# A graph network on one core: the last hidden state summed with its residual on TensorE, and a new order of all engines

## The chip, the core and the metric

The kernel runs on one core of a Trainium2 chip. A core has four compute engines with a queue each: TensorE (PE, matrix products, with weight loads listed apart as PEld), VectorE (DVE), ScalarE (ACT) and GpSimd (POOL). SyncE (SP) issues the DMA transfers. Each engine works its instructions strictly in the order in which the program lists them and waits on semaphores for the others. Products land in PSUM, eight banks of 128 x 512 fp32 numbers; everything else lives in SBUF. The metric is the device time of one execution in microseconds (us), the median of several runs.

## What is computed

The reference, cut to what matters; `x` is 32 x 512 x 128, `adj` 512 x 512, all fp32:

```python
def _chebyshev(adj, x, order):                 # order 3
    def step(carry, _):
        nxt = jnp.einsum('ij,bjc->bic', adj, carry)
        return (nxt, nxt)
    ...
def _L0_gnn_ref(x_1, adj0, adj1, weight_1):
    parts = [x_1[..., None], _chebyshev(adj0, x_1, 3), _chebyshev(adj1, x_1, 3)]
    x_all = jnp.concatenate(parts, axis=3)
    return jnp.einsum('bnik,iok->bno', x_all, weight_1)

def step(h, _):                                # layer 1, five times
    m_in = jnp.einsum('nm,bmd->bnd', in_matrix, h)
    m_out = jnp.einsum('nm,bmd->bnd', out_matrix, h)
    av = jnp.concatenate([m_in, m_out], axis=-1)
    u3 = h @ u3_w.T + u3_b
    z = jax.nn.sigmoid(av @ w3_w.T + w3_b + u3)
    r = jax.nn.sigmoid(av @ w4_w.T + w4_b + u3)
    hv = jnp.tanh(av @ w5_w.T + w5_b + (r * h @ u5_w.T + u5_b))
    h = (1.0 - z) * h + z * hv
    return (h, None)

x = _layernorm(x + _L0_gnn_ref(x, adj, adj, weight_1), axis=-1)
x = _layernorm(x + _L1_gnn_ref(x, adj, adj, ...), axis=-1)
```

Layer 0 adds a graph convolution to `x` and normalises over the 128 channels; its result is called h0. Layer 1 starts from h0, makes five gated steps, adds the last hidden state h to h0 and normalises again. Both adjacency matrices are the same one, so the two halves of each gate's weight are added beforehand.

## The kernel before

The 32 batches go through in 16 pairs q = 0 to 15, two batches b each; pairs are independent. `pair(q, key0)` builds all the work of a pair: `layer0`, five steps s, then the sum with h0, the second normalisation and the store.

A batch's hidden state exists in two layouts. `hT` has the channels on the 128 partitions and the 512 nodes along the free axis: the gates use it. `X` has the nodes on the partitions: it is the stationary operand of the adjacency product, and the layout of h0 and of the output. After each step h is turned from `hT` to `X`. `turn` does it by a 32 x 32 block transpose on DVE (into a `v` tile), eight small DMAs on SP's queue to DRAM (`d`) and one back. Where `by_dma` is false, four transposes of 128 x 128 on PE (`transposes`, into a PSUM bank `bt`) do it. By `ON_PE = {14: 1, 15: 3}` that is the last step of pair 14 and the last three steps of pair 15.

`pair_product` makes the adjacency product of both batches with seven products instead of eight, out of sums that POOL and ACT prepare in an `S` tile; `seven` lists the products and their evictions. `gates` does one step for one batch: r from w4, z from w3, the candidate from w5 and u5. For r and z, DVE adds bias and u3 in PSUM (L705, L712) and ACT applies the sigmoid (L707, L714); DVE forms r*h (L708), ACT applies the tanh (L721). Then h + z*(hv - h) is formed in three steps: DVE subtracts (L724), DVE multiplies (L726), and POOL adds into `hT` (L729). With `quick` true, which is all steps of the last `QUICK = 2` pairs, DVE does that add.

After the last step of a pair that is turned by DMA, POOL adds `X` to h0 (L792). Where PE turned it, DVE adds the PSUM bank to h0 (L797) and the bank is free. `norm` then takes four groups of 128 channels a batch: DVE makes moments (L283, L284), POOL the power -0.5 and the shift in four small instructions (L287 to L290), ACT scales in place (L293); SP stores (L804).

The order of every engine's instructions comes from a list scheduler, `Plan`. Each piece of work names its engine, a booked duration, what it comes after, which buffers it takes and gives back, and a key. Whenever an engine is free in the plan's clock, it takes the ready piece with the lowest key whose buffers are free. Keys are a pair's start `KEYS[q]`, plus 20 for each step, plus small offsets within a step (product 0, u3 5, gates 10, turn 15, final norm 17). `OVERLAP` shortens the booked occupation of DVE, ACT and POOL and lengthens the lateness of the result by as much, so that a result's time stays while the engine is free sooner. `slots` holds the number of buffers of each kind; `inside` bounds the pairs that have been entered.

The booked time of four PE transposes is 0.44 us, and of a product of two 128-column matmuls in layer 0 (L565) also 0.44.

Of the kernel before, what the change touches and what calls it, by code (L numbers as in the profile page):

```python
# [10 lines left out]
AF = mybir.ActivationFunctionType  # L11
# [3 lines left out]
P = 128  # L15
NK = 4
# [7 lines left out]
QUICK = 2  # L24
KEYS = [20.0, 58.0, 80.0, 112.0, 148.0, 180.0, 208.0, 240.0, 272.0, 304.0, 334.0, 366.0, 396.0, 426.0, 464.0, 478.0]
# [18 lines left out]
class Plan:  # L44
# [6 lines left out]
    OVERLAP = {"DVE": 0.08, "ACT": 0.1, "POOL": 0.04}  # L51
# [6 lines left out]
    def __call__(self, engine, us, emit, after=(), take=(), give=(), key=0.0, late=None):  # L58
        late = self.LATE[engine] if late is None else late
        overlap = min(self.OVERLAP.get(engine, 0.0), us / 2)  # L60
        us, late = us - overlap, late + overlap
        op = Op(engine, us, emit, [a for a in after if a is not None], take, give, key, late)
        self.ops.append(op)
        return op
# [62 lines left out]
def gnn_resnorm_kernel(  # L127
# [26 lines left out]
    def tiles(tag, n, shape=(P, N), pool=work):  # L154
# [7 lines left out]
        tT=tiles("tT", 5),  # L162
        U=tiles("U", 2, (P, NK, 2, P)),
        Y=tiles("Y", 4, (P, 2, NK, P)),
        h0=tiles("h0", 4, (P, 2, NK, P)),
        hT=tiles("hT", 8),
        X=tiles("X", 4),
        uT=tiles("uT", 6),
        rh=tiles("rh", 3),
        z=tiles("z", 4),  # L170
        m=tiles("m", 5),
        S=tiles("S", 2, (P, 7, H, P)),
        v=tiles("v", 7),
        two=[None] * 3,
        inside=[None] * 7,
# [98 lines left out]
    def norm(n, name, src_of, dst_of, after, give, key):  # L274

        mv = small.tile([P, n, 2], F32, tag="mv", name=f"mv_{name}")
        rstd = small.tile([P, n], F32, tag="rstd", name=f"rstd_{name}")
        shift = small.tile([P, n], F32, tag="shift", name=f"shift_{name}")
        got = []

        def moments(i):
            st = small.tile([P, 6], F32, tag="st", name=f"st_{name}_{i}")
            nc.vector.bn_stats(st, src_of(i))  # L283
            nc.vector.bn_aggr(mv[:, i, :], st)  # L284

        def power():
            nc.gpsimd.tensor_scalar(rstd, mv[:, :, 1], EPS, None, ALU.add)  # L287
            nc.gpsimd.tensor_scalar(shift, mv[:, :, 0], -1.0, None, ALU.mult)
            nc.gpsimd.tensor_tensor(rstd, rstd, mhalf[:, :n], ALU.pow)
            nc.gpsimd.tensor_tensor(shift, shift, rstd, ALU.mult)  # L290

        def apply(i):
            nc.scalar.activation(  # L293
                dst_of(i), src_of(i), AF.Identity, bias=shift[:, i : i + 1], scale=rstd[:, i : i + 1]
            )

        for i in range(n):
            got.append(plan("DVE", 0.48, lambda i=i: moments(i), after=after, key=key))
        p = plan("POOL", 1.75, power, after=got, key=key)
        over = []  # L300
        for i in range(n):
            last = i == n - 1
            over.append(
                plan("ACT", 0.5, lambda i=i: apply(i), after=[p] + over, give=give if last else [], key=key)
            )
        return over
# [163 lines left out]
    def fit(t, turned):  # L470
        return t.rearrange("p k (s d) -> p k s d", d=R) if turned else t
# [222 lines left out]
    def gates(name, m, h, after, u_done, quick, key):  # L694

        uT = f"uT{name}"
# [16 lines left out]
        t = plan("DVE", 0.75, emit, after=[p2, u_done], give=[("uT", uT)], key=key + 0.5)  # L713
        emit = lambda: nc.scalar.activation(plan[z], plan[pz], AF.Sigmoid)  # L714
        zs = plan("ACT", 0.59, emit, after=[t], give=[("bank", pz)], key=key + 0.5)
# [6 lines left out]
        t = plan("ACT", 0.66, emit, after=[p4], key=key + 0.8)  # L722

# [4 lines left out]
        engine, us = (nc.vector, 0.69) if quick else (nc.gpsimd, 1.27)  # L728
        emit = lambda: engine.tensor_tensor(plan[h], plan[z], plan[h], ALU.add)  # L729
        return plan("DVE" if quick else "POOL", us, emit, after=[t], give=[("z", z)], key=key + 0.8)  # L730

    def pair(q, key0):
# [6 lines left out]
        for s in range(STEPS):  # L739
# [29 lines left out]
            for b in range(2):  # L769
                nm = f"{name}_{b}"  # L770
                Xb = f"X{nm}"
                d = gates(nm, f"m{nm}", h[b], got[b], u_done[b], q >= NP - QUICK, key + 10)
# [5 lines left out]
                else:  # L778
                    bn = f"bt{nm}"
                    emit = lambda bn=bn, hb=h[b]: transposes(plan[bn], lambda k: plan[hb][:, chunk(k)])  # L780
                    take = [("bank", bn)] + ([] if last else [("X", Xb)])
                    t = plan("PE", 0.44, emit, after=[d] + read[b], take=take, give=give, key=key + 15)
                    if not last:
                        emit = lambda bn=bn, Xb=Xb: nc.scalar.copy(plan[Xb], plan[bn])
                        t = plan("ACT", 0.59, emit, after=[t], give=[("bank", bn)], key=key + 15)
# [5 lines left out]
                if by_dma:  # L791
                    emit = lambda b=b, X_new=X_new, y=y: nc.gpsimd.tensor_tensor(  # L792
                        fit(y(), True), X_new(b), fit(y(), True), ALU.add
                    )
                    t = plan("POOL", 1.27, emit, after=[t], give=[("X", Xb)], key=key + 17)
                else:
                    emit = lambda y=y, bn=bn: nc.vector.tensor_tensor(  # L797
                        y(), plan[bn].rearrange("p (k c) -> p k c", k=NK), y(), ALU.add
                    )
                    t = plan("DVE", 0.69, emit, after=[t], give=[("bank", bn)], key=key + 17)  # L800
# [68 lines left out]
```

## Time and profile before

| | |
|---|---|
| median of 3 runs | 1525.26 us (1524.48 to 1526.72) |
| the profiled execution's own time | 1526.63 us |
| span, first to last instruction | 1524.5 us |
| PE matmul / weight loads, busy | 1498.4 / 1034.4 us |
| DVE / ACT / POOL busy | 975.6 / 753.5 / 750.6 us |
| mean granted PE clock | 0.995 |
| chain that ended last, share by engine | PE 90%, DVE 4%, DMA 2% |
| DMA, mean | 85 GB/s, 31.3% of 16 engines |

The profile is of one execution. Its span leaves out some 2 us around the first and last instruction, so that its own time, not the median, belongs to it. L numbers are lines of the kernel. A row of the timeline gives the start from the beginning of the span, the duration, engine, line, operation, output and inputs, the number of instructions merged, and in brackets the engine's idle time before with what ended it. Matmuls are pipelined: a single one's duration is longer than the distance from its start to the next, and the latter is what it costs a busy PE. In a waits row stand the waiting engine and line, what it waited for, total us, times, and the longest.

### The profile page before, as it was taken

Reading aid. Unit: us, or ns where it says so; the run is one execution under the profiler, and the core shown is the slowest. Engines: PE = TensorE matmul, PEld = TensorE weight load, DVE = VectorE, ACT = ScalarE, POOL = GpSimd, SP = SyncE. Lnnn points to the kernel's source line nnn. Section 1 sums busy time; section 2 is a strip of 40 time slices with the busy share of each in tenths; the row PEclk is TensorE's granted clock in tenths of the full one; section 3 lists DMA queues with packets and bytes.
Section 4 is the critical chain, followed back from the end, with each engine's and each line's share of the span. In section 5 each row is a group of like instructions: output and inputs, shape, how many; then the busy total and the mean of one; then the engine's idle time right before and its main releaser. Section 6 shows DMA issues by size and latency. Waiting matters only on the chain.

```text
span 1524.5 us, 20210 instructions
## 1 busy us (share of the span) xinstructions
PE 1498.4 (98%) x6216; PEld 1034.4 (68%) x6216; DVE 975.6 (64%) x2068; ACT 753.5 (49%) x1610; POOL 750.6 (49%) x1068
## 2 busy tenths in 40 slices
PE   8999999999999999999999999999999999999995
PEld 7876676666766766666676766676675776665563
DVE  5457566766666766566666566666676456766766
ACT  3454545454454455455545454555445435554554
POOL 4654354655564554464645464564553464543222
PEclk9999999999999999999999999999999999999998
DMA  3221333243333324243333433224233033233310
GB/s 116 62 71 48 85 90 98 81 108 101 82 99 97 90 79 109 69 105 83 88 92 98 105 103 77 77 82 132 83 84 99 26 83 84 57 102 90 84 42 28
DMA packets 162140, 129.23 MB, mean 85 GB/s; under 512 B 18544, under 2 KB 127088, under 8 KB 162032
## 3 DMA queue, kind: packets, MB, share of 16 engines
q1 hardware_dynamic: 162032, 127.93, 31.3%
q8 instruction: 50, 0.82, 0.2%
q14 instruction: 58, 0.48, 0.1%
HBM read 64.95 MB, written 62.91 MB: 84 GB/s over the span
## 4 chain that ended last, share of the span: by engine, by line
PE 90%; DVE 4%; DMA 2%; SPq 2%; ACT 1%; POOL 1%; issue 1%; ACTq 0%; POOLq 0%; DVEq 0%
PE bank L487 35%; PE bank L700 32%; PE bank L746 8%; PE bank L624 6%; PE bank L565 6%; DMA X<-d 1%; SPq L315 1%; PE bank L423 1%; PE bank L272 1%; DVE bank L724 1%; DVE st L283 0%; DVE z L726 0%; POOL h L792 0%; DVE mv L284 0%; ACT h L293 0%
## 5 line engine op out<-in xcount | busy, mean ns | idle before, releaser
L487 PE MATMUL bank<-T,S 128*128 128x256 f32 x1400 | 345.4, 380 | 0.3 <-ACT m L348 0.2
L487 PEld LDWEIGHTS bank<-T,S 128*128 128x128 f32 x1400 | 264.3, 190 | 99.2 <-ACT m L348 48.7
L729 POOL TENSOR_TENSOR hT<-z,hT 128x512 f32<-128x512 f32 x140 | 177.4, 1270 | 279.0 <-DVE z L726 274.8
L487 PE MATMUL bank<-at,S 128*128 128x256 f32 x880 | 226.8, 381 | 3.8 <-ACT S L467 1.4
L348 ACT COPY m<-bank 128x256 f32<-128x256 f32 x320 | 118.4, 370 | 216.4 <-PE bank L487 215.3
L487 PEld LDWEIGHTS bank<-at,S 128*128 128x128 f32 x880 | 165.3, 190 | 76.6 <-issue 39.7
L352 DVE TENSOR_TENSOR m<-bank,m 128x256 f32<-128x256 f32 x240 | 100.0, 417 | 171.8 <-PE bank L487 106.5
L724 DVE TENSOR_TENSOR bank<-bank,hT 128x512 f32<-128x512 f32 x160 | 110.0, 692 | 117.7 <-ACT bank L721 116.7
L746 PE MATMUL bank<-hT,u3s 128*128 128x512 f32 x320 | 159.8, 593 | 0.0
L700 PE MATMUL bank<-m,w3s 128*128 128x512 f32 x320 | 158.4, 593 | 0.0
L700 PE MATMUL bank<-m,w4s 128*128 128x512 f32 x320 | 158.4, 593 | 0.0
L700 PE MATMUL bank<-m,w5s 128*128 128x512 f32 x320 | 157.9, 593 | 0.0
L700 PE MATMUL bank<-rh,u5s 128*128 128x512 f32 x320 | 157.1, 594 | 0.7 <-DVE rh L708 0.7
L751 ACT ACTIVATE uT<-bank,ub3s 128x512 f32<-128x512 f32 x160 | 109.6, 686 | 81.4 <-PE bank L746 81.1
L705 DVE SCALAR_TENSOR_TENSOR bank<-bank,b4s,uT 128x512 f32<-128x512 f32 x160 | 119.8, 752 | 46.2 <-PE bank L700 42.4
L721 ACT ACTIVATE bank<-bank,hv_b 128x512 f32<-128x512 f32 x160 | 105.4, 660 | 86.6 <-PE bank L700 85.8
L707 ACT ACTIVATE bank<-bank 128x512 f32<-128x512 f32 x160 | 92.9, 582 | 109.2 <-DVE bank L705 108.6
L712 DVE SCALAR_TENSOR_TENSOR bank<-bank,b3s,uT 128x512 f32<-128x512 f32 x160 | 118.8, 751 | 15.5 <-PE bank L700 14.1
L714 ACT ACTIVATE z<-bank 128x512 f32<-128x512 f32 x160 | 94.8, 595 | 62.3 <-DVE bank L712 60.8
L708 DVE TENSOR_TENSOR rh<-bank,hT 128x512 f32<-128x512 f32 x160 | 107.6, 680 | 16.5 <-ACT bank L707 16.0
L323 DVE STREAM_TRANSPOSE v<-hT 128x512 f32<-128x512 f32 x152 | 105.3, 698 | 10.2 <-POOL hT L729 9.1
L726 DVE TENSOR_TENSOR z<-bank,z 128x512 f32<-128x512 f32 x160 | 108.3, 682 | 2.2
(119 smaller groups left out, 2178.5 us busy)
## 6 DMA issues: line engine op xcount, KB each, us to landing
d<-v SPq DMA_DIRECT2D x832, 64.0 KB, 1.8
X<-d SPq DMA_DIRECT2D x152, 256.0 KB, 2.9
v<-d SPq DMA_DIRECT2D x56, 256.0 KB, 2.8
xg<-in_x SPq DMA_DIRECT2D x32, 256.0 KB, 3.0
out<-h SPq DMA_DIRECT2D x32, 256.0 KB, 2.1
at<-in_adjT SPq DMA_DIRECT2D x4, 256.0 KB, 5.0
U<-in_w SPq DMA_DIRECT2D x1, 448.0 KB, 6.6
z<-in_w SPq DMA_DIRECT2D x3, 128.0 KB, 6.4
```

The lines of the kernel that those rows point to most:

```text
L348: return "ACT", COPY[cols], lambda src: nc.scalar.copy(dst(i, j), src)
L487: nc.tensor.matmul(dst, lhsT=left[:, k, :], rhs=right[:, k, :], start=(first and k == 0), stop=(last and k == H - 1), skip_group_check=True,)
L700: mm = lambda dst, w, src, first, last: nc.tensor.matmul(plan[dst], lhsT=w, rhs=plan[src], start=first, stop=last)
L705: emit = lambda: nc.vector.scalar_tensor_tensor(plan[pr], plan[pr], b4s, plan[uT], ALU.add, ALU.add)
L708: emit = lambda: nc.vector.tensor_tensor(plan[rh], plan[pr], plan[h], ALU.mult)
L712: emit = lambda: nc.vector.scalar_tensor_tensor(plan[pz], plan[pz], b3s, plan[uT], ALU.add, ALU.add)
L721: emit = lambda: nc.scalar.activation(plan[ph], plan[ph], AF.Tanh, bias=hv_b)
L724: emit = lambda: nc.vector.tensor_tensor(plan[ph], plan[ph], plan[h], ALU.subtract)
L726: emit = lambda: nc.vector.tensor_tensor(plan[z], plan[ph], plan[z], ALU.mult)
L729: emit = lambda: engine.tensor_tensor(plan[h], plan[z], plan[h], ALU.add)
L746: emit = lambda bn=bn, hb=h[b]: nc.tensor.matmul(plan[bn], lhsT=u3s, rhs=plan[hb], start=True, stop=True)
L751: emit = lambda bn=bn, uT=uT: nc.scalar.activation(plan[uT], plan[bn], AF.Identity, bias=ub3s)
```

## The change

In the last step of pairs 14 and 15 (`quick` now means the last step where PE turns h), h is no longer formed in `hT`. It is split as (1 - z)*h + z*hv. ACT makes 1 - z as a sigmoid of the negated argument into a tile of the kind `rh`; DVE multiplies it with h in place (the kept part) and the tanh with z (the new part). The new function `finish` sums three things in a PSUM bank: h0 by plain matmuls with the identity as the stationary operand, then the kept and the new part by plain matmuls with the part as the stationary operand and the identity moving, which turns them. The normalisation reads the bank and writes h0's tile, from where it is stored. For the very last batch (`by_dve`), DVE subtracts the mean and scales, and POOL makes two of its four instructions. The other steps of pairs 14 and 15 have their final add on POOL, as all other pairs have. `OVERLAP` is gone, the keys of eleven pairs differ, and so do most buffer counts; so the order of every engine is drawn up anew, over the whole kernel.

```diff
@@ -21,8 +21,7 @@
 NR = P // R
 STEPS = 5
 ON_PE = {14: 1, 15: 3}
-QUICK = 2
-KEYS = [20.0, 58.0, 80.0, 112.0, 148.0, 180.0, 208.0, 240.0, 272.0, 304.0, 334.0, 366.0, 396.0, 426.0, 464.0, 478.0]
+KEYS = [20.0, 58.0, 80.0, 110.0, 158.0, 194.0, 216.0, 246.0, 282.0, 312.0, 338.0, 366.0, 396.0, 432.0, 468.0, 480.0]
 LONG = 20.0
 FIRST = 2
 EPS = 1e-5
@@ -48,7 +47,6 @@
 
 
     LATE = {"PE": 0.2, "DVE": 0.1, "ACT": 0.1, "POOL": 0.1, "SP": 0.0, "-": 0.0}
-    OVERLAP = {"DVE": 0.08, "ACT": 0.1, "POOL": 0.04}
 
     def __init__(self, slots):
         self.slots = slots
@@ -57,8 +55,6 @@
 
     def __call__(self, engine, us, emit, after=(), take=(), give=(), key=0.0, late=None):
         late = self.LATE[engine] if late is None else late
-        overlap = min(self.OVERLAP.get(engine, 0.0), us / 2)
-        us, late = us - overlap, late + overlap
         op = Op(engine, us, emit, [a for a in after if a is not None], take, give, key, late)
         self.ops.append(op)
         return op
@@ -159,20 +155,20 @@
         d=tiles("d", 6, (NR, R, NR, P), dram),
         xg=tiles("xg", 2, (P, 2, NK, P)),
         xT=tiles("xT", 4),
-        tT=tiles("tT", 5),
-        U=tiles("U", 2, (P, NK, 2, P)),
-        Y=tiles("Y", 4, (P, 2, NK, P)),
-        h0=tiles("h0", 4, (P, 2, NK, P)),
-        hT=tiles("hT", 8),
-        X=tiles("X", 4),
-        uT=tiles("uT", 6),
-        rh=tiles("rh", 3),
-        z=tiles("z", 4),
-        m=tiles("m", 5),
-        S=tiles("S", 2, (P, 7, H, P)),
-        v=tiles("v", 7),
+        tT=tiles("tT", 4),
+        U=tiles("U", 3, (P, NK, 2, P)),
+        Y=tiles("Y", 2, (P, 2, NK, P)),
+        h0=tiles("h0", 5, (P, 2, NK, P)),
+        hT=tiles("hT", 9),
+        X=tiles("X", 5),
+        uT=tiles("uT", 5),
+        rh=tiles("rh", 4),
+        z=tiles("z", 3),
+        m=tiles("m", 7),
+        S=tiles("S", 3, (P, 7, H, P)),
+        v=tiles("v", 5),
         two=[None] * 3,
-        inside=[None] * 7,
+        inside=[None] * 10,
     )
     plan = Plan(slots)
 
@@ -271,7 +267,7 @@
         for k in range(NK):
             nc.tensor.transpose(dst[:, chunk(k)], src_of(k), ident)
 
-    def norm(n, name, src_of, dst_of, after, give, key):
+    def norm(n, name, src_of, dst_of, after, give, key, by_dve=False):
 
         mv = small.tile([P, n, 2], F32, tag="mv", name=f"mv_{name}")
         rstd = small.tile([P, n], F32, tag="rstd", name=f"rstd_{name}")
@@ -285,24 +281,30 @@
 
         def power():
             nc.gpsimd.tensor_scalar(rstd, mv[:, :, 1], EPS, None, ALU.add)
-            nc.gpsimd.tensor_scalar(shift, mv[:, :, 0], -1.0, None, ALU.mult)
+            if not by_dve:
+                nc.gpsimd.tensor_scalar(shift, mv[:, :, 0], -1.0, None, ALU.mult)
             nc.gpsimd.tensor_tensor(rstd, rstd, mhalf[:, :n], ALU.pow)
-            nc.gpsimd.tensor_tensor(shift, shift, rstd, ALU.mult)
+            if not by_dve:
+                nc.gpsimd.tensor_tensor(shift, shift, rstd, ALU.mult)
 
         def apply(i):
+            if by_dve:
+                nc.vector.tensor_scalar(
+                    dst_of(i), src_of(i), mv[:, i, 0:1], rstd[:, i : i + 1], ALU.subtract, ALU.mult
+                )
+                return
             nc.scalar.activation(
                 dst_of(i), src_of(i), AF.Identity, bias=shift[:, i : i + 1], scale=rstd[:, i : i + 1]
             )
 
         for i in range(n):
             got.append(plan("DVE", 0.48, lambda i=i: moments(i), after=after, key=key))
-        p = plan("POOL", 1.75, power, after=got, key=key)
+        p = plan("POOL", 1.2 if by_dve else 1.75, power, after=got, key=key)
+        engine, us = ("DVE", 0.35) if by_dve else ("ACT", 0.5)
         over = []
         for i in range(n):
-            last = i == n - 1
-            over.append(
-                plan("ACT", 0.5, lambda i=i: apply(i), after=[p] + over, give=give if last else [], key=key)
-            )
+            ends = give if i == n - 1 else []
+            over.append(plan(engine, us, lambda i=i: apply(i), after=[p] + over, give=ends, key=key))
         return over
 
     def turn(src_of, dst_of, name, after, key, take=(), give=()):
@@ -693,6 +695,7 @@
 
     def gates(name, m, h, after, u_done, quick, key):
 
+
         uT = f"uT{name}"
         pr, pz, ph = (f"b{g}{name}" for g in "rzh")
         rh, z = f"rh{name}", f"z{name}"
@@ -710,9 +713,9 @@
 
         p2 = plan("PE", 0.86, lambda: mm(pz, w3s, m, True, True), after=[p], take=[("bank", pz)], key=key + 0.5)
         emit = lambda: nc.vector.scalar_tensor_tensor(plan[pz], plan[pz], b3s, plan[uT], ALU.add, ALU.add)
-        t = plan("DVE", 0.75, emit, after=[p2, u_done], give=[("uT", uT)], key=key + 0.5)
+        pre_z = plan("DVE", 0.75, emit, after=[p2, u_done], give=[("uT", uT)], key=key + 0.5)
         emit = lambda: nc.scalar.activation(plan[z], plan[pz], AF.Sigmoid)
-        zs = plan("ACT", 0.59, emit, after=[t], give=[("bank", pz)], key=key + 0.5)
+        zs = plan("ACT", 0.59, emit, after=[pre_z], give=[] if quick else [("bank", pz)], key=key + 0.5)
 
         emit = lambda: mm(ph, w5s, m, True, False)
         p3 = plan("PE", 0.86, emit, after=[p2], take=[("bank", ph)], give=[("m", m)], key=key + 0.7)
@@ -720,14 +723,50 @@
         p4 = plan("PE", 0.86, emit, after=[p3, r], give=[("rh", rh)], key=key + 0.8)
         emit = lambda: nc.scalar.activation(plan[ph], plan[ph], AF.Tanh, bias=hv_b)
         t = plan("ACT", 0.66, emit, after=[p4], key=key + 0.8)
+        if quick:
+
+            rest = f"rest{name}"
+            emit = lambda: nc.scalar.activation(plan[rest], plan[pz], AF.Sigmoid, scale=-1.0)
+            k = plan("ACT", 0.59, emit, after=[pre_z, zs], take=[("rh", rest)], give=[("bank", pz)], key=key + 0.6)
+            emit = lambda: nc.vector.tensor_tensor(plan[h], plan[rest], plan[h], ALU.mult)
+            k = plan("DVE", 0.69, emit, after=[k, r], give=[("rh", rest)], key=key + 0.7)
+            emit = lambda: nc.vector.tensor_tensor(plan[z], plan[ph], plan[z], ALU.mult)
+            return k, plan("DVE", 0.69, emit, after=[t, zs], give=[("bank", ph)], key=key + 0.8)
 
         emit = lambda: nc.vector.tensor_tensor(plan[ph], plan[ph], plan[h], ALU.subtract)
         t = plan("DVE", 0.69, emit, after=[t], key=key + 0.8)
         emit = lambda: nc.vector.tensor_tensor(plan[z], plan[ph], plan[z], ALU.mult)
         t = plan("DVE", 0.69, emit, after=[t, zs], give=[("bank", ph)], key=key + 0.8)
-        engine, us = (nc.vector, 0.69) if quick else (nc.gpsimd, 1.27)
-        emit = lambda: engine.tensor_tensor(plan[h], plan[z], plan[h], ALU.add)
-        return plan("DVE" if quick else "POOL", us, emit, after=[t], give=[("z", z)], key=key + 0.8)
+        emit = lambda: nc.gpsimd.tensor_tensor(plan[h], plan[z], plan[h], ALU.add)
+        return plan("POOL", 1.27, emit, after=[t], give=[("z", z)], key=key + 0.8)
+
+    def finish(q, b, name, h, parts, h0_of, after, key, done):
+
+        bn, z = f"bt{name}", f"z{name}"
+        y = lambda k: plan[bn][:, chunk(k)]
+
+        def summed(tile, turned, first, last):
+            for k in range(NK):
+                a = tile(k)
+                nc.tensor.matmul(
+                    y(k),
+                    lhsT=a if turned else ident,
+                    rhs=ident if turned else a,
+                    start=(first and k == 0),
+                    stop=last,
+                    skip_group_check=True,
+                )
+
+        keep, new = parts
+        emit = lambda: summed(lambda k: h0_of(b)[:, k, :], False, True, False)
+        t = plan("PE", 0.44, emit, after=list(after), take=[("bank", bn)], key=key)
+        emit = lambda: summed(lambda k: plan[h][:, chunk(k)], True, False, False)
+        t = plan("PE", 0.44, emit, after=[t, keep], give=[("hT", h)], key=key)
+        emit = lambda: summed(lambda k: plan[z][:, chunk(k)], True, False, True)
+        t = plan("PE", 0.44, emit, after=[t, new], give=[("z", z)], key=key)
+        over = norm(NK, f"1_{2 * q + b}", y, lambda k: h0_of(b)[:, k, :], [t], [("bank", bn)], key + 10, q == NP - 1 and b == 1)
+        emit = lambda: nc.sync.dma_start(out[2 * q + b].rearrange("(p k) c -> p k c", k=NK), h0_of(b))
+        done.append(plan("SP", 0.36, emit, after=over, key=key + 10, late=2.0))
 
     def pair(q, key0):
 
@@ -769,7 +808,12 @@
             for b in range(2):
                 nm = f"{name}_{b}"
                 Xb = f"X{nm}"
-                d = gates(nm, f"m{nm}", h[b], got[b], u_done[b], q >= NP - QUICK, key + 10)
+                quick = last and not by_dma
+                d = gates(nm, f"m{nm}", h[b], got[b], u_done[b], quick, key + 10)
+                if quick:
+                    finish(q, b, nm, h[b], d, h0_of, read[b], key + 15, done)
+                    h_done.append(list(d))
+                    continue
                 h_done.append([d])
                 give = [("hT", h[b])] if last else []
                 if by_dma:
@@ -778,26 +822,19 @@
                 else:
                     bn = f"bt{nm}"
                     emit = lambda bn=bn, hb=h[b]: transposes(plan[bn], lambda k: plan[hb][:, chunk(k)])
-                    take = [("bank", bn)] + ([] if last else [("X", Xb)])
+                    take = [("bank", bn), ("X", Xb)]
                     t = plan("PE", 0.44, emit, after=[d] + read[b], take=take, give=give, key=key + 15)
-                    if not last:
-                        emit = lambda bn=bn, Xb=Xb: nc.scalar.copy(plan[Xb], plan[bn])
-                        t = plan("ACT", 0.59, emit, after=[t], give=[("bank", bn)], key=key + 15)
+                    emit = lambda bn=bn, Xb=Xb: nc.scalar.copy(plan[Xb], plan[bn])
+                    t = plan("ACT", 0.59, emit, after=[t], give=[("bank", bn)], key=key + 15)
                 after.append([t])
                 if not last:
                     continue
 
                 y = lambda b=b: h0_of(b)
-                if by_dma:
-                    emit = lambda b=b, X_new=X_new, y=y: nc.gpsimd.tensor_tensor(
-                        fit(y(), True), X_new(b), fit(y(), True), ALU.add
-                    )
-                    t = plan("POOL", 1.27, emit, after=[t], give=[("X", Xb)], key=key + 17)
-                else:
-                    emit = lambda y=y, bn=bn: nc.vector.tensor_tensor(
-                        y(), plan[bn].rearrange("p (k c) -> p k c", k=NK), y(), ALU.add
-                    )
-                    t = plan("DVE", 0.69, emit, after=[t], give=[("bank", bn)], key=key + 17)
+                emit = lambda b=b, X_new=X_new, y=y: nc.gpsimd.tensor_tensor(
+                    fit(y(), True), X_new(b), fit(y(), True), ALU.add
+                )
+                t = plan("POOL", 1.27, emit, after=[t], give=[("X", Xb)], key=key + 17)
                 i = 2 * q + b
                 y_of = lambda k, y=y: y()[:, k, :]
                 over = norm(NK, f"1_{i}", y_of, y_of, [t], [], key + 17)
```

## The prediction

> **What bounds the kernel now.** I read the page's table of engines first, then TensorE's own waits, then the timeline of the end.
>
> The table of engines, with the clock's slices:
> ```profile
> PE 1498.4 (98%) x6216; PEld 1034.4 (68%) x6216; DVE 975.6 (64%) x2068; ACT 753.5 (49%) x1610; POOL 750.6 (49%) x1068
> ...
> PEclk9999999999999999999999999999999999999998
> ```
> TensorE (PE) is busy 98% of 1524.5 us at the full clock, no other engine over 64%. A new matmul therefore costs its whole time unless it falls into one of PE's gaps. What PE's matmuls wait for:
> ```profile
> PE bank L272 <- DMA xg<-in_x: 4.7, 2, 3.6
> PE bank L272 <- DVE hT L729: 3.3, 1, 3.3
> PE bank L487 <- ACT S L467: 1.4, 2, 1.0
> PE bank L487 <- DVE tT L352: 1.2, 3, 0.6
> PE bank L487 <- DVE m L352: 1.1, 2, 0.6
> PE bank L624 <- DVE v L349: 0.9, 2, 0.6
> PE bank L700 <- DVE rh L708: 0.7, 1, 0.7
> PE bank L565 <- ACT Y L348: 0.5, 1, 0.5
> PE bank L487 <- ACT m L348: 0.2, 1, 0.2
> ```
> Columns: total us, times, longest. The first row is the start (input loads), the second the end. The other seven sum to 6.0 us: all that a better order in between could win. The end, from the timeline:
> ```profile
> 1495.96 1.04 PE L272 MATMUL bank<-ident,hT 128*128 128x128 f32 x8
> 1496.83 1.03 PE L487 MATMUL bank<-T,S 128*128 128x256 f32 x4
> ...
> 1505.43 1.88 PE L700 MATMUL bank<-rh,u5s 128*128 128x512 f32 x4
> 1506.82 1.21 ACT L721 ACTIVATE bank<-bank,hv_b 128x512 f32<-128x512 f32 x2
> 1507.49 1.30 DVE L724 TENSOR_TENSOR bank<-bank,hT 128x512 f32<-128x512 f32 x2 [1.83 <-ACT bank L721]
> 1508.70 1.28 DVE L726 TENSOR_TENSOR z<-bank,z 128x512 f32<-128x512 f32 x2
> 1509.89 1.28 DVE L729 TENSOR_TENSOR hT<-z,hT 128x512 f32<-128x512 f32 x2
> 1510.63 1.97 PE L272 MATMUL bank<-ident,hT 128*128 128x128 f32 x8 [3.32 <-DVE hT L729]
> ```
> Columns: start, duration. PE issues without a stop up to the last u5 matmul; four 512-column halves at 0.43 us put the end of its stream, U, at 1507.15. The span ends 17.35 us after U, through three DVE steps for each of two batches, transposes, an add, moments, POOL's power, ACT's scaling and the store.
>
> **The change part by part.** Only the last step of pairs 14 and 15 reaches the new branch: two pairs of two batches, four in all.
>
> *PE, added.* A plain matmul shows in this trace as two instructions, a transpose as one. The price of each is read from starts:
> ```profile
> 37.99 1.06 PE L565 MATMUL bank<-wt,S 128*128 128x128 f32 x8
> 38.88 1.03 PE L487 MATMUL bank<-T,xg 128*128 128x256 f32 x4
> ```
> Wait-free, eight 128-column instructions take 0.89 us, 0.112 each; eight transposes take 1496.83 - 1495.96 = 0.87, 0.109 each. finish() makes three sums of four plain matmuls a batch: 3 x 8 x 0.112 = 2.69 us, for one set of four transposes, 0.44. The planner books 0.44 for each sum, half of the row. Pair 14's are 2 x (2.69 - 0.44) = **+4.5 us**; in 1455 to 1507 PE has one gap, 0.3 us, so nothing covers them.
>
> The Trainium skill, "TensorE: Matmul & The Clock Gate", Terms, speaks against putting plain matmuls in a transpose's place: it calls transpose mode four times faster for FP32. The rows here say twice (0.89 to 0.44). By the rule a sum would take an estimated 1.75 us and pair 14's term would be +9.6.
>
> *The end, pair 15.* After U, by durations of before:
> - Tanh of both ends at 1508.03, U+0.9. One DVE multiply for a batch (L726's) instead of three steps: done at U+1.05 and U+1.65.
> - Last sum of each, 0.9: U+1.95 and U+2.85, PE free until then.
> - Moments, 0.40 apart, four a batch: with 0.15 from PE to DVE, U+2.1 to 3.7 and to 5.3. That PSUM is their source: the SBUF row is taken; 512-column DVE rows reading PSUM (0.68 to 0.75) and not reading it (0.68) differ by at most 10%, 0.3 us here.
> - POOL: batch 0's chain of four 1.82 (as at 1515.01 to 1516.83), to 5.6; batch 1's two instructions 1.35, to 7.05.
> - DVE's four scalings of 128x128: no such row. From 0.18 (the aggregate row) to 0.40 (128x128 tensor_tensor, L236); 0.3 taken, nearest to the stats row of 0.27: 1.2, to 8.35.
> - Store to the end, as before (1520.80 to 1524.5): 3.7, U+12.05.
>
> That is 5.3 less. But pair 15's h0 and keep sums, 4 x 0.9 = 3.6, also stand somewhere. Before U they push U; after U, PE is idle for 1.05 us, one sum's worth. Three before U: -5.3 + 2.7 = -2.6. All after: the last sums end at 4.5 and 5.4, the end at U+14.6, -2.75. All four before: -1.7. I take **-2.7**. The clock fell to half at 1509.5 in before, 2.4 us into PE's wait, and the transposes at the end came 0.21 us apart. With sums in the gap it should not fall; if it does, the two last sums cost up to +1.8.
>
> *ACT and DVE in that step.* A second sigmoid per batch, 0.59, with ACT back to back from 1505.10 to 1508: 0 to +1.2 ahead of pair 15's tanh, +0.5 taken. The kept product (0.68 on DVE) lies in DVE's idle 1.83 us before L724; without that cover its sum comes later, by up to 0.7. DVE's subtract, h add and read-out add go (0.69 each); only pair 15's are on the path, counted above.
>
> *Step adds of pairs 14 and 15 go back to POOL*, 16 of 20: 1.27 instead of 0.68. A POOL add starts as soon as the product is there, without DVE's queue: for the step of pair 14 ending at 1466 it would be 0.2 and 0.5 us later. Queued behind it on SP are eight puts and two fetches; the X copy they feed is what the single 0.3 us gap at 1475 waits for. From -0.3 (DVE relieved) to +1.6 (0.4 in each of four rounds), +0.3 taken.
>
> *Banks.* A sum's bank is held from the h0 sum to the last scaling, some 10 us, where transposes held it under 2. Pair 15's gates use six of eight banks then, pair 14's two sums the others: 0 to +1. With the second sigmoid's hold on pz, 0 taken.
>
> *The new order, keys and counts.* SP's booked times do not change, so the waits for X landing (1.4 + 0.2) can stay. Longer DVE and ACT bookings put more PE work between producer and consumer, which could end the other waits: floor -6.0. Against it, fewer v, Y, tT, uT and z (5, 2, 4, 5, 3) can make PE wait where it does not now. No row bounds that; the longest of the waits above is 1.0, and one in every eighth of 96 products (80 steps, 16 of layer 0) would be +12, the ceiling. I take +1.7, nearer to before, since its buffers hardly ever ran out either.
>
> Sum: 4.5 - 2.7 + 0.5 + 0.3 + 1.7 = **+4.3 us**. On the profiled span, 1528.8. That execution took 1526.63, 1.4 above the median of 1525.26; on the median, 1529.5.
>
> **The rivals.**
> 1. *Better order wins* (ends faster). With everything local at +2.6, the order must win more than 5.7 of the 6.0 us of waits, or some at the start too, for a gain of 0.2%. For: more S, m and X. Against: that is nearly all there is. At its best, 1525.3 + 2.6 - 6.0 = 1522; with 2 us of the start's 4.7, 1520.
> 2. *Wash.* The order wins 1 to 5 us and the sums cost what I say: 1524 to 1528. A smaller cost of the sums (the planner's 0.44 each) gives the same: pair 14's term 1.8, end about -4.4, with +2.5 of the rest the total is 0: 1525.
> 3. *Buffers starve PE*: five v tiles hold turns, layer-0 outputs and raw fetches together; an SP put behind a full v stops every later one. Some 8 to 25 us of new PE waits, 1534 to 1552. For: SP is strictly in order and waits 546.6 us in total for L323. Against: those waits hid.
>
> **How the numbers follow.** The forecast (+3 to +9) has 0.43, rival 3 0.12, wash 0.28, better order 0.17. Measurement tells 0.2%, 3 us. Slower 0.43 + 0.12 = 0.55, same 0.28, faster 0.17. The range from 1519.5 (better order nearly whole) to 1539 (rival 3's lower part) leaves about one in ten. The forecast's own range is 1528 to 1535.
>
> **What would show it.** New matmul rows of 96 instructions at 0.112 start to start, in groups of eight 0.89 apart; 16 transposes fewer; last u5 at about 1512 to 1515 from the span's start, and 12 to 15 us from it to the end; four DVE scalings there at 0.2 to 0.4; PE's waits away from start and end between 0 and 12 us. It is wrong if a sum shows four instructions, if the clock halves before the last sums, or if PE's other waits move by more than 5 us.

## The result, and the profile after

The changed kernel takes 1518.7 us (median of 5 runs, 1516.3 to 1520.0) against 1525.3 before (5 runs, 1524.5 to 1531.3): ratio 0.9947, 95% interval 0.9926 to 0.9969. It is faster by 0.5%, where I forecast slower by 0.3%. The profiled execution took 1518.7 us, with a span of 1516.9.

The page's table of engines and the clock's slices of the changed kernel:
```profile
PE 1502.4 (99%) x6296; PEld 1044.2 (69%) x6296; DVE 968.9 (64%) x2048; ACT 750.4 (49%) x1610; POOL 767.1 (51%) x1082
...
PEclk9999999999999999999999999999999999999999
```
PE has 80 matmul instructions more and is busy longer, in a shorter span. The clock no longer falls before the last matmuls. What its matmuls wait for (waiting line, releaser, total us, times, longest):
```profile
PE bank L268 <- DMA xg<-in_x: 4.4, 2, 3.8
PE bank L489 <- ACT S L469: 1.1, 1, 1.1
PE bank L489 <- ACT tT L350: 0.5, 1, 0.5
PE bank L268 <- POOL hT L740: 0.4, 1, 0.4
```
Where before had seven kinds of wait between start and end, there are three, each met once. The end, from PE's timeline:
```profile
1502.45 1.88 PE L703 MATMUL bank<-rh,u5s 128*128 128x512 f32 x4
1504.17 1.05 PE L751 MATMUL bank<-h,ident 128*128 128x128 f32 x8
1505.06 1.06 PE L751 MATMUL bank<-ident,hT 128*128 128x128 f32 x8
1505.96 1.06 PE L751 MATMUL bank<-ident,z 128*128 128x128 f32 x8
1506.85 1.06 PE L751 MATMUL bank<-ident,hT 128*128 128x128 f32 x8
1507.74 1.06 PE L751 MATMUL bank<-ident,z 128*128 128x128 f32 x8
```
The last u5 group starts at 1502.45, where before had it at 1505.43: 3 us earlier, although seven of the twelve sums now stand before it. The five others follow without a gap.

**Where the time went.** I take the distance from each matmul's start to the next and subtract the distance of a full PE (0.430, 0.216, 0.112 us for 512, 256, 128 columns). What is left is time that PE lost; the time up to the first matmul is counted to the start. "Middle" is from 100 us to the last u5 matmul, "end" from that stream's end to the span's end.

| us | before | after | difference |
|---|---|---|---|
| lost up to 100 us | 11.2 | 11.1 | -0.1 |
| lost in the middle | 8.7 | 0.5 | -8.2 |
| matmul work up to the last u5 | | | +5.4 |
| end | 17.4 | 12.7 | -4.7 |
| span | 1524.5 | 1516.9 | -7.6 |

The work is seven sums of 0.89 less two sets of transposes of 0.44. So the new ending costs about what it returns (+5.4 and -4.7), and the gain is that PE hardly waits any more in the middle. Which part of the new order does that (the long bookings, the counts, the keys), or any redrawing at all, is what the runs are for.

The scheduler's own clock helps to read them. It is no measurement: it is the time that the program reckons with while it draws up the order, and it says where PE would idle if every booking were right. In that clock PE idles 0.1 us in the middle of before, and lost 8.7 on the chip: all its waits were unplanned. In that of the changed kernel it idles 2.4 us, and lost 0.5.

### The profile page after: what moved, and what is told of

Same layout as the page of the kernel before. It is cut to its first block, busy times and chain, and to the rows that moved or that the text cites. A ratio compares the mean times of both kernels' runs of the same rounds, so it can differ in the third digit from the quotient of the medians.

```text
span 1516.9 us, 20326 instructions
## 1 busy us (share of the span) xinstructions
PE 1502.4 (99%) x6296; PEld 1044.2 (69%) x6296; DVE 968.9 (64%) x2048; ACT 750.4 (49%) x1610; POOL 767.1 (51%) x1082
## 4 chain that ended last, share of the span: by engine, by line
PE 97%; DMA 1%; DVE 1%; POOL 1%; SPq 0%; issue 0%; ACT 0%; ACTq 0%; POOLq 0%; DVEq 0%
PE bank L489 38%; PE bank L703 36%; PE bank L785 9%; PE bank L567 6%; PE bank L626 6%; PE bank L425 1%; PE bank L751 1%; PE bank L268 1%; SPq L317 0%; DMA xg<-in_x 0%; DMA d<-v 0%; DMA v<-d 0%; DVE v L325 0%; POOL rstd L286 0%; DMA X<-d 0%
## 5 line engine op out<-in xcount | busy, mean ns | idle before, releaser
L740 POOL TENSOR_TENSOR hT<-z,hT 128x512 f32<-128x512 f32 x156 | 197.6, 1272 | 279.6 <-DVE z L738 277.7
L708 DVE SCALAR_TENSOR_TENSOR bank<-bank,b4s,uT 128x512 f32<-128x512 f32 x160 | 119.9, 752 | 44.2 <-PE bank L703 37.2
L738 DVE TENSOR_TENSOR z<-bank,z 128x512 f32<-128x512 f32 x156 | 104.9, 681 | 1.8
```

What stands on the lines that cost most here:

```text
L708: emit = lambda: nc.vector.scalar_tensor_tensor(plan[pr], plan[pr], b4s, plan[uT], ALU.add, ALU.add)
L740: emit = lambda: nc.gpsimd.tensor_tensor(plan[h], plan[z], plan[h], ALU.add)
```

## The experiments

Theories: the long bookings alone; the buffer counts; the keys, or a lucky draw; the ending.

**1. New order, old ending.** The code of before with three settings of after:
```diff
-    OVERLAP = {"DVE": 0.08, "ACT": 0.1, "POOL": 0.04}     (and its two lines)
-KEYS, slots of before
+KEYS, slots of after
```


> The changed kernel's bookings, keys and buffer counts with the old ending (quick adds on DVE, transposes, add out of PSUM, normalisation on ACT). My ledger of the two traces says that the new order won 8.2 us of PE waits between 100 us and the last u5 matmul, and that the new ending cost 5.4 us of PE work ahead of that point and won 4.6 us after it: about +0.8. If so, this kernel has under 2 us of such waits and takes 1516 to 1519 us, the changed kernel's time or a little less. If the ending is what made the change faster, it takes 1522 to 1526. If any redrawing of the order moves the waits by several us, its waits lie anywhere between 0 and 10 us.

Measured: 1515.6 us, ratio to before 0.994 (0.9922 to 0.9958); lost in the middle 1.4 us. PE's waits:
```profile
PE bank L269 <- DMA xg<-in_x: 4.1, 2, 3.7
PE bank L269 <- DVE hT L726: 3.4, 1, 3.4
PE bank L484 <- ACT S L464: 1.8, 2, 1.1
PE bank L484 <- ACT tT L345: 0.5, 1, 0.5
```
The wait for the last h (second row) is back with the old ending, and the waits in the middle are still gone. The whole gain is the order's. The time is just under the expected 1516 to 1519. This kernel is below the changed one, by 3.1 us of the medians; the two ranges overlap a little (1514.7 to 1518.0 against 1516.3 to 1520.0).

**2. New ending, old order.** The code of after with OVERLAP, KEYS and slots of before (the diff of experiment 1 the other way round).

> The kernel before with its shortened bookings, keys and counts, and only the new ending. By the ledger PE's waits in the middle stay at 7 to 10 us and the time is 1525 to 1528 us. If the ending is the gain: 1517 to 1521, with the waits unchanged. If redrawing alone moves the waits: anywhere from 1517 to 1530, following its waits.

Measured: 1526.3 us, ratio 1.0005 (0.9995 to 1.0015); lost in the middle 9.5 us. The last u5 stream ends 4.6 us later than in before, the end is 4.7 us shorter (12.7). By itself the ending is worth nothing here.

**3. Short bookings put back.**
```diff
+    OVERLAP = {"DVE": 0.08, "ACT": 0.1, "POOL": 0.04}
...
+        overlap = min(self.OVERLAP.get(engine, 0.0), us / 2)
+        us, late = us - overlap, late + overlap
```


> The changed kernel with the shortened bookings of DVE, ACT and POOL put back; keys, counts and ending as changed. If the longer bookings are what ended PE's waits, they come back to 6 to 9 us and the time is 1524 to 1528 us. If the buffer counts or the keys ended them, they stay under 2 us and the time is 1517 to 1520.

Measured: 1520.3 us, ratio 0.9966 (0.9955 to 0.9977); lost in the middle 3.0 us, not 6 to 9 and not under 2, and the time is between both expected ranges. By the losses the bookings are one part and counts and keys hold another; the times alone (1517.5 to 1521.4 against 1516.3 to 1520.0) overlap.

**4. New ending in pair 15 alone.**
```diff
-ON_PE = {14: 1, 15: 3}
+ON_PE = {15: 3}
```


> The changed kernel with the new ending in pair 15 alone; pair 14's last h is turned by DMA, added by POOL and normalised in SBUF like all pairs before it. It leaves out pair 14's 48 matmul instructions of 0.112 us, 5.4 us of PE time. If PE is full there and these sums lay on its path: 1512 to 1515 us, the last u5 matmul 5 us earlier. If they lay in time that PE would have waited anyway: 1517 to 1520. If the DMA turn makes PE or the end wait: above 1520.

Measured: 1516.7 us, ratio 0.9945 (0.9926 to 0.9964). The last u5 stream ends 3.8 us earlier than in the changed kernel: 4.5 us of sums less before it (pair 14's 5.4 are gone, but both h0 sums of pair 15 now stand ahead of it instead of one), 0.9 us less lost before 100 us, and 1.5 us more lost in the middle (2.0). The end grew to 14.3, because PE now waits 1.2 us for pair 15's kept part. Pair 14's sums did lie on PE's path, but 2 us of the 5.4 came through (medians; the ranges overlap), between my ranges; the lower one assumed an otherwise unchanged order, and the edit redraws it.

**5. Old buffer counts in the changed kernel.**
```diff
-        U 3, Y 2, h0 5, hT 9, X 5, uT 5, rh 4, z 3, m 7, S 3, v 5, tT 4, inside 10
+        U 2, Y 4, h0 4, hT 8, X 4, uT 6, rh 3, z 4, m 5, S 2, v 7, tT 5, inside 7
```


> The changed kernel with the buffer counts of before; long bookings, keys and ending as changed. In the scheduler's own clock PE then idles 40.5 us after 100 us (3.2 with the new counts), for want of buffers. If the counts are a needed half of the change, PE waits 10 to 40 us on the chip and the time is 1526 to 1555 us. If the long bookings alone end the waits, because the chip is faster than they say and the planned idle time closes up, PE's waits stay under 3 us and the time is 1517 to 1521.

Measured: 1545.1 us, ratio 1.013 (1.011 to 1.015); lost in the middle 28.3 us. PE's waits between 100 and 1490 us, the first rows:
```profile
PE bank L567 <- ACT Y L350: 3.6, 7, 0.7
PE bank L567 <- ACT U L350: 2.7, 3, 1.7
PE bank L489 <- ACT m L350: 1.9, 4, 0.5
PE bank L703 <- ACT m L350: 1.8, 1, 1.8
```
With the new counts the same bookings, keys and ending are planned with 2.4 us of holes, so it is for want of buffers that the scheduler finds no work for PE here. A booking's result time is the same long or short, so a long one does not itself hold a buffer longer; but pieces come later where engines are booked longer. In the order of experiment 6 against that of before, a U tile is held 57 us on average instead of 44 and a uT tile 26 instead of 20 (m, rh and tT are not held longer). The chip closes part of the planned idle time (28.3 of 39.7 us left), not all: an order that is drawn with holes is executed with holes.

**6. Long bookings alone, in before.**
```diff
-    OVERLAP = {"DVE": 0.08, "ACT": 0.1, "POOL": 0.04}     (and its two lines)
```


> The kernel before with the long bookings alone; its counts, keys and ending. In the scheduler's clock PE idles 27.7 us after 100 us, 4.0 of them at the end (4.3 and 4.0 before the edit). If long bookings alone suffice: PE's waits in the middle fall from 8.7 to under 3 us, 1517 to 1520 us. If they need the new counts: waits of 8 to 25 us, 1525 to 1543 us.

Measured: 1529.3 us, ratio 1.0031 (1.002 to 1.0041): slower. Lost in the middle 13.8 us (planned 22.0).

**7. New counts alone, in before.** The `slots` lines of after, nothing else.

> The kernel before with the new buffer counts alone; short bookings, old keys and ending. If the counts carry most of the gain, as the changed kernel with short bookings suggests (3.0 us of waits), PE's waits fall to 2 to 4 us and the time is 1518 to 1521 us; the scheduler's clock has 5 us of idle time in the middle here, which could stand on top. If short bookings set the waits: 7 to 10 us, 1524 to 1528.

Measured: 1525.9 us, ratio 0.9998 (0.9987 to 1.0009). Lost in the middle 9.5 us, planned 4.8: with short bookings the unplanned waits come on top. The larger gain that I expected from counts did not show.

**8. Old keys in the changed kernel.**
```diff
-KEYS = [20.0, 58.0, 80.0, 110.0, 158.0, 194.0, ...
+KEYS = [20.0, 58.0, 80.0, 112.0, 148.0, 180.0, ...
```


> The changed kernel with the keys of before; the scheduler's clock has 6.0 us of idle time after 100 us instead of 3.2. If bookings and counts carry the gain: PE's waits 0 to 3 us, 1517 to 1521 us. If the keys do, or the changed kernel's order is a lucky draw: waits of 6 to 10 us, 1523 to 1528.

Measured: 1519.8 us, ratio 0.9968 (0.9952 to 0.9984); lost in the middle 2.7 us, planned 5.1. The gain does not hang on the new keys alone: with these, the one other set tried, 0.32 of the 0.53% stay (the two ranges overlap).

**9. DVE scaling on top of experiment 1.** Both batches of pair 15:
```diff
+                nc.vector.tensor_scalar(
+                    dst_of(i), src_of(i), mv[:, i, 0:1], rstd[:, i : i + 1], ALU.subtract, ALU.mult
+                )
...
-                over = norm(NK, f"1_{i}", y_of, y_of, [t], [], key + 17)
+                over = norm(NK, f"1_{i}", y_of, y_of, [t], [], key + 17, q == NP - 1)
```


> The kernel of the first experiment (new order, old ending) with one more edit: both batches of pair 15 are scaled by DVE out of mean and power, and POOL makes two instead of four small instructions. From the old ending's rows: POOL's chain ends 0.9 us earlier and four scalings take 1.3 instead of 2.0. If the middle stays as it was: 1513.5 to 1515 us, 1 to 2 under the first experiment's 1515.6. If DVE's queue delays the second batch's moments by the first's scaling: 1515.5 to 1517.

Measured: 1515.8 us, ratio 0.9938 (0.9923 to 0.9953). The end is 1.3 us shorter (14.9 against 16.2), as worked out; but the profiled execution lost 2.8 us in the middle, 1.4 more than that of experiment 1, so the median shows nothing. It lies in my second range, but not for its reason: DVE began to scale after the moments of both batches. A gain of 1 us is not to be told from one execution's waits to the next.

**10. Two sums in pair 15, on top of experiment 9.** In place of pair 15's last transposes:
```diff
+                            nc.tensor.matmul(
+                                plan[bn][:, chunk(k)],
+                                lhsT=plan[tile][:, chunk(k)],
+                                rhs=ident,
...
```


> As the run before it, and in pair 15 alone h is split into the kept and the new part, which PE sums and turns in two plain sums a batch (16 matmul instructions of 0.112 us, booked at 0.9 us a sum) in place of one set of transposes; h0 is added by DVE as before, not by PE. After the tanh the path has one DVE step instead of three a batch, 2.4 us less, and 0.9 us of sums more; PE gets 2.7 us more work, of which 1.8 can stand before the last u5 matmul. If the kept sums fall into PE's wait for the tanh: 1512 to 1514 us. If they stand on PE's path: 1514 to 1516.

Measured: 1516.6 us, ratio 0.9942 (0.9926 to 0.9959); end 13.6 us, lost in the middle 2.6. Both kept sums stand after the last u5, as hoped, and the end is 1.3 us shorter than experiment 9's. It is no faster, and above both expected ranges: the last u5 stream itself ends 1.8 us later, for its profile lost 2.0 us more before 100 us, around the input loads (10.9 against 8.9). Whether it is better with a start like experiment 9's stays open.

**11. The sums booked at what they cost.**
```diff
-        t = plan("PE", 0.44, emit, ...        (three times in finish)
+        t = plan("PE", 0.9, emit, ...
```


> The changed kernel with its twelve sums booked at 0.9 us, what they cost on the chip, instead of 0.44. If the wrong booking costs something (sums put ahead of pair 15's gates), the last u5 matmul comes earlier against the sums after it and the time falls to 1515 to 1518. If PE is full in any case, the same work in another order: 1517.5 to 1520, waits in the middle under 2 us.

Measured: 1519.1 us, ratio 0.9958 (0.9943 to 0.9973); lost in the middle 1.4 us. The booking of the sums made no difference.

**12. Short bookings with new counts and keys, old ending.** Experiment 1 with OVERLAP and its two lines kept.

> The first experiment's kernel (new counts, new keys, old ending) with the short bookings of before: against that one it differs by the bookings alone, against the seventh by the keys alone. In the scheduler's clock PE idles 0.4 us in the middle here. In all eleven kernels so far the chip's waits in the middle were above the scheduler's idle time with short bookings (by 2.5 to 8.6 us) and at or below it with long ones. If that holds, the waits are 3 to 9 us and the time is 1517 to 1523 us, 1.5 to 7 above the first experiment's 1515.6. If counts and keys do all of it: waits under 2 us, 1515 to 1516.5.

Measured: 1520.5 us, ratio 0.9957 (0.9944 to 0.9971); lost in the middle 3.7 us, planned 0.4. PE's waits between 100 and 1490 us:
```profile
PE bank L487 <- POOL S L474: 0.8, 1, 0.8
PE bank L487 <- POOL rstd L289: 0.6, 1, 0.6
PE bank L487 <- ACT m L348: 0.4, 1, 0.4
```
and of experiment 1 in the same stretch:
```profile
PE bank L484 <- ACT S L464: 0.7, 1, 0.7
```
With all else equal, the kernel with long bookings is 4.8 us faster by the medians (1520.5 to 1515.6; the ranges 1519.2 to 1521.6 and 1514.7 to 1518.0 don't meet). That is too much to credit to the bookings: the two were measured in different sessions, on different chips, and before itself had a median of 1526.84 in this one and 1525.95 in that of experiment 1. By the ratios to before (0.9957 and 0.9940) the difference is 2.6 us, and their intervals overlap. Of the two spans' difference of 4.5, 2.3 is time lost in the middle; the rest is the start (10.9 to 9.3 lost) and the end (16.9 to 16.2), which the bookings need not have caused. Experiment 3 against the changed kernel says much the same with the new ending: 2.9 us by the ratios, 2.5 lost in the middle.

**All together.** Planned: PE's idle time in the middle in the scheduler's clock. Lost: on the chip, in one profiled execution.

| kernel | bookings | counts | keys | ending | planned | lost | median us |
|---|---|---|---|---|---|---|---|
| before | short | old | old | old | 0.1 | 8.7 | 1525.3 |
| 2 | short | old | old | new | 0.9 | 9.5 | 1526.3 |
| 7 | short | new | old | old | 4.8 | 9.5 | 1525.9 |
| 12 | short | new | new | old | 0.4 | 3.7 | 1520.5 |
| 3 | short | new | new | new | 0.5 | 3.0 | 1520.3 |
| 6 | long | old | old | old | 22.0 | 13.8 | 1529.3 |
| 5 | long | old | new | new | 39.7 | 28.3 | 1545.1 |
| 8 | long | new | old | new | 5.1 | 2.7 | 1519.8 |
| after | long | new | new | new | 2.4 | 0.5 | 1518.7 |
| 1 | long | new | new | old | 2.9 | 1.4 | 1515.6 |
| 4 | long | new | new | pair 15 | 4.9 | 2.0 | 1516.7 |

In all five kernels with short bookings the chip lost more than was planned (2.5 to 8.6 us more). In all six here with long ones, and in 9, 10 and 11, it lost less (planned 2.9, 2.9 and 2.4; lost 2.8, 2.6 and 1.4). That much is shown: with short bookings PE, strictly in order, comes to instructions whose operands are not there yet, where the plan had them there; with long ones planned holes are partly closed. Long bookings need the new counts, or the scheduler plans holes too large to close (5 and 6). By the ratios to before, each taken with before in the same session: counts and keys win 0.43% with short bookings (12, about 6.6 us), long bookings alone cost 0.31% (6, 4.7 us), and all three win 0.60% (1, 9.2 us). So counts and keys are the larger part, long bookings add some 2 to 3 us to it, and without the counts they harm.

The short bookings are not too short for what an instruction costs its engine. In before's trace, one after the other without a wait, 512-column multiplies on DVE (L708, L726) start 0.60 us apart (booked 0.61 short, 0.69 long), its sums of bias and u3 (L705) 0.66 (0.67, 0.75), ACT's sigmoids 0.49 (0.49, 0.59), its tanh 0.585 (0.56, 0.66) and POOL's adds 1.23 (1.23, 1.27). The short ones are nearly exact; the long ones are slack. What the slack can be good for shows in before's longest wait in the middle, PE's at 1396.94 for an S. The chain of releasers behind it:
```profile
1391.62 4.84 DMA X<-d
1396.48 0.41 ACT S L467
```
This fetch (a turn by DMA is four puts, eight for the pair, and one fetch a batch) took 4.84 us from issue to landing, where the median of its kind is 2.9 and the plan books 3.15 (0.35 and 2.8). Other waits (at 367.37, 907.69 and 1089.26) stand behind POOL's add L792 and the moments after it in DVE's queue. That slack in the engines' bookings works by taking up such late results is argued from these rows; no run tested it.

Not settled: which of the thirteen counts carry it (five were cut, and no run cut or raised one alone), and why counts and keys lower the unplanned losses under short bookings (lost less planned: before 8.6, experiment 7 4.7, experiment 12 3.3).

## Why the prediction was wrong

**The new order: this step failed.** The prediction took +1.7 us, between -6.0 and +12; the middle moved by -8.2. Two errors are in it.

*The floor.* I read the waits view's 6.0 us as all that a better order could win. It is less than PE lost. In before's timeline of PE:
```profile
1394.91 1.02 PE L700 MATMUL bank<-m,w3s 128*128 128x512 f32 x2
1396.94 1.13 PE L487 MATMUL bank<-at,S 128*128 128x256 f32 x4 [1.00 <-ACT S L467]
```
Two 512-column instructions keep PE for 0.86 us, so the next could start at 1395.77; it started at 1396.94, 1.17 later. The view says 1.00, since a matmul's row is 0.16 us longer than its stream. From 100 to 1490 us the view lists nine waits with 4.7 us in before; by starts it was 8.7. The nine were 6.1, 0.16 each more than listed, and 23 shorter stops of 0.05 to 0.30 us, 2.6 us together, are not in the view at all.

*The value.* I placed it near before "since its buffers hardly ever ran out either", and held the smaller counts against the change. The lines of waits named results that came late (S, m, tT, rh, v), not buffers that were missing, and I had written myself that longer bookings put more work between producer and consumer. Runs 1 and 12 show that the new order takes most of these waits away, with short bookings (3.7 lost) and more so with long ones (1.4). Runs 5 and 6 show my rival 3 (buffers starve PE, +1.3% and +0.3%) for long bookings with the old counts. The rival that I gave 0.17, better order wins, was the right one, and its reason ("more S, m and X") is among the counts that changed, though no run raised those alone. Even its best case, 1520 to 1522, lay above the 1518.7 measured, since its floor was too high.

**The ending: right in its size, in part by luck.** Terms and measurements: 2.69 us of sums a batch at 0.112 start to start (eight start 0.89 apart, 1504.17 to 1505.06). What the Trainium skill, "TensorE: Matmul & The Clock Gate", Terms, states of transpose mode, four times faster for FP32, is not borne out by these rows: one matmul costs two instructions of 0.112 against one of 0.109. From the stream's end to the end of the span I had 12.05 to 14.6 us, measured 12.7 with five sums inside. The path there was another than mine, though. I had batch 0's chain of four on POOL first and DVE's scalings of the last batch at the end. On the chip DVE's batch came first and was scaled by 1511.80; the other batch's chain on POOL followed, and ACT ended the scaling at 1513.98:
```profile
1512.47 1.51 ACT L296 ACTIVATE h<-bank,shift,rstd 128x128 f32<-128x128 f32 x4 [6.50 <-POOL shift L288]
```
With U the end of the last u5 stream (1504.17 here), that is U+9.8, where I had U+8.35 for three sums ahead of U; from there to the end it took 2.9 us instead of 3.7.

My local sum without the order was +2.6 us. Measured with the new order, 1 to after: +2.8 us of the spans, +3.1 of the medians; with the old order, before to 2: no difference of the spans, ratio 1.0005. The two agree less well than that looks: by sums and end alone it is +1.9 with the new order (+5.4 and -3.5) and +0.7 with the old one, and the rest is time lost at the start and in the middle (1 lost 1.8 us less than the changed kernel before 100 us), which the ending need not have caused. So +2.6 was somewhat high. ACT's extra sigmoids let the second tanh end 1.1 us after the stream instead of 0.9: +0.2 for +0.5 taken. No wait for a PSUM bank to come free shows in PE's rows of the middle.

**POOL adds in pairs 14 and 15: hidden,** but for one wait: PE's 0.4 us for POOL's hT at 1447.9, against +0.3 taken.

**The clock: right.** With sums in the gap it stays full until 1514.18, 5.5 us after the last sum's stream, when no matmul is left. In before it fell at 1509.72 (not 1509.5, as I had read), and the last eight transposes ran 0.21 us apart.

**DVE scaling: right in its size.** Four took 1.33 us, against 1.2 taken; they were not on the path that ended last.

**Signs to watch.** Of those named, the rows, the spacing, the end and the scalings came as said; the last u5, forecast for 1512 to 1515, started at 1502.45 and its stream ended at 1504.17, which gave the error away. PE's other waits, by the view that I had named, went from 6.0 to 2.0 us, inside the 5 that I allowed; by starts the middle moved by 8.2. This sign hung on the same view as the floor.

## What to carry to other kernels

When a list scheduler writes the order, compare its planned idle time with the chip's: if the chip waits where the plan does not, the plan has no room for what comes late. Here bookings longer than the measured cost won some 2 to 3 us on top of new counts and keys, and lost 4.7 without them, so try both together. Measure PE's lost time by starts, not by the idle time in a view, before saying what a better order can bring at most. An ending that moves work onto a full engine pays only for what it saves after that engine's last product: here 4.7 us for 5.4, and the old ending with the new order was by the medians the fastest kind of kernel tried (1515.6 and 1515.8 us, 0.6% under before).

## What the runs showed of the hardware

A DVE `tensor_scalar` of 128x128 with two per-partition operands costs more out of PSUM than out of SBUF: four merged took 1.33 us in the changed kernel and 1.10 in experiment 9, 0.06 each.
```profile
1510.47 1.33 DVE L292 TENSOR_SCALAR h<-bank,mv,rstd 128x128 f32<-128x128 f32 x4
```
```profile
1508.26 1.10 DVE L293 TENSOR_SCALAR h<-h,mv,rstd 128x128 f32<-128x128 f32 x4
```
That fits the Trainium skill, "VectorE: DVE Perf Modes", Why PSUM operands drop a tier: its 2×_2P mode needs both SBUF read ports, PSUM has one, and fp32 out of PSUM is capped at 1×. At that page's 0.96 GHz, one element a cycle instead of two would be an estimated 0.07 us more for 128 elements. With one tile size the rows cannot tell a rate from a fixed cost of reading PSUM.

The same order of instructions does not lose the same time twice. Experiments 1 and 9 have PE's instructions in one and the same order; in the middle they lost 1.4 and 2.8 us, 1.0 and 1.6 of it ahead of matmuls that waited for ACT's copies (`S`) of an X that a DMA had brought.
